# Graph transformer layer pair on one core: reciprocals of the first two graphs due at once, dots of W and a and the check of adj at other times, last unit but one by way of DRAM

## The chip, the cores and the metric

One core of one Trainium2 chip. The metric is the device time of one execution in microseconds (us). All runs quoted are in the fast state. Medians are of the fast runs of one kernel; a ratio is the mean time of one kernel's fast runs over the mean of the other's of the same rounds, so it is not quite the ratio of the medians quoted beside it. Every kernel below gave the right result.

Names: PE is TensorE, DVE VectorE, ACT ScalarE, POOL GpSimd, SP the engine whose queue starts most DMAs. (b, j) is unit j (two heads of eight) of graph b. L648 is line 648 of the kernel. In the profile's names pd is the tile of the sums of the exponentials, ps the scores, po the exponentials times v, pn transposes, pe the product for the diagonal of graph attention, pg graph attention itself; x_, qz_ and y_ with q, k, v, w or y behind them are products with Wq, Wk, Wv, Wo (w) and W (y). Where the prediction says "products of W" at 146.7 us it means those with Wo.

## The reference, cut to what matters

32 graphs of 512 nodes with 512 features go through masked attention and then through graph attention; all is float32.

```python
h = relu(layernorm(x))
q, k, v = h @ Wq + bq, h @ Wk + bk, h @ Wv + bv          # 8 heads of 64
attn = softmax(q k^T / 8 + (1 - adj) * -1e9)
x = x + (attn v) @ Wo + bo
h = relu(layernorm(x)) @ W
e = leaky_relu(h a1 [:, None] + h a2 [None, :]) * adj
x = x + elu(softmax(e) @ h + beta * h)
```

## The kernel before: the parts that the change touches

PE works through a fixed order of parts for each graph. DVE's smaller jobs are not placed by hand: they are put on a list with an earliest time, a deadline and a cost, and a clock that the program keeps while it is built decides where they go. What comes out is a fixed order on each engine.

```python
def pe(us):                      # after each piece of PE work
    clock["pe"] += us
    till = clock["pe"] + (1.0 if at_ends[0] else 0.4)
    while True:
        due = [i for i, (_, t, _) in enumerate(ends) if t <= till]
        fits = [(by, i) for i, (_, t, cost, _, by) in enumerate(spare)
                if max(clock["dve"], t) + cost <= till]
        if due:     ends.pop(due[0])[2]()        # pieces of ACT and POOL that follow
        elif fits:  run_spare(min(fits)[1])      # the piece of DVE with the earliest deadline
        else:       return

def later(key, wait, by, cost, fn):   # earliest time, deadline, cost
    now = max(clock["dve"], clock["pe"])
    spare.append((key, now + wait, cost, fn, now + by))
```

Four kinds of such jobs matter. The check of adj (is every entry 0 or 1?), the dots of W and a (W a1 and W a2, which go to all partitions by way of a row in DRAM), and the reciprocals of the softmax sums:

```python
for t in range(T):                                   # in masks()
    later("bad", 120.0, 200.0, 1.35, lambda t=t: other(t))
...
for c in range(C):                                   # in row_constants()
    for o in range(2):
        later("wa", 40.0, 50.0, 0.75, lambda g=g, c=c, o=o, ar=ar: dot(g, c, o, ar))
...
def finish(b, j, st):
    need("rd")
    if b == B - 1 and j >= NP - 2:
        return finish_last(b, j, st)
    pd = psum.tile([P, N], F32, name=f"pd_{b}_{j}", tag="pd")[:, :H]
    ...                                              # PE: sums of the exponentials into pd
    rd = wtile([P, N], f"rd_{b}_{j}", "rd", 1)       # ONE buffer
    rq = rd[:, :H]

    def divide():
        nc.vector.reciprocal(rq, pd)                 # L638
        then("rd", spread)

    def spread():
        d = dram.tile([2, N], F32, name=f"rd_{b}_{j}", tag="rd")
        nc.scalar.activation(pd, rq, AF.Copy, accum_out=rsum[:, b, j : j + 1])   # L644
        nc.scalar.dma_start(d.rearrange("s (k q) -> (s k) q", k=2), rq[0:P:32, :])
        for s in range(2):
            nc.sync.dma_start(rd[s * HD : (s + 1) * HD, :], d[s : s + 1, :].to_broadcast([HD, N]))
        then("rd", lambda: nc.gpsimd.tensor_tensor(o, o, rd, op=ALU.mult), 6.0)  # L648
    ...
    later("rd", 0.0, gap(b, (j + 1) % NP) - 4.0 if (b, j) != (0, NP - 1) else 0.0, 1.7, divide)
```

The last unit of all (`finish_last`) makes its reciprocals without the trip through DRAM, with two instructions of 1.75 us on DVE. Before, the last but one did so too.

The fourth kind is graph attention's logits: after the eight dots of hn (L767) of a graph, a row goes through DRAM, and DVE makes four logits (L787, L790) and three sums of them (L801). PE needs the last sum for the diagonal (`pe`, part "D"):

```python
nc.vector.scalar_tensor_tensor(z, row, s12[:, 1, k : k + 1], adjT[:, k, :], op0=ALU.add, op1=ALU.mult)  # L787
nc.vector.scalar_tensor_tensor(z, z, ALPHA, z, op0=ALU.mult, op1=ALU.max)                               # L790
...
nc.vector.tensor_tensor(st["as"], st["at"][0] if k == 1 else st["as"], z, op=ALU.add)                   # L801
```

## Time and profile before

| | before |
|---|---|
| median of 3 runs | 3560.45 us (3560.12 to 3561.3) |
| span of the profiled execution | 3561.3 us |
| PE, DVE, ACT, POOL busy | 98, 76, 41, 39% |
| single waits of PE over 3 us | 6.8 (qz_q), 5.1 (pe, end), 4.9 (qz_k), 4.4 (pd), 3.6 (pd, end), 3.3 (qz_y, end) |

PE is the bound over nearly the whole span. All that a change of order can win lies at the two ends, at 150 to 250 us and from 3440 us on. The lines are in the prediction.

### The profile page before, as it was taken

The page shows a single profiled execution, that of the slowest core. Times are in us where ns is not written, and L with a number is a line of the kernel's source. Part 1 is how long each engine was busy: PE and PEld are TensorE (multiplying, and loading weights), DVE is VectorE, ACT ScalarE, POOL GpSimd, SP SyncE. Part 2 cuts the span into 40 slices and gives each one's busy share as a digit, 9 for nine tenths or more (in the row PEclk, how much of TensorE's full clock was granted, in tenths as well). Part 3 has the DMA queues.
Part 4 walks back from the last instruction along what each step waited for, and adds up shares of the span by engine and source line. Part 5 has one row for each costly group of instructions (what it writes and reads, how often), then busy time and mean ns, then how long its engine had stood idle before and what let it go on. Part 6 is the DMA issues. An engine that isn't in the chain of part 4 may idle for free.

```text
span 3561.3 us, 64126 instructions
## 1 busy us (share of the span) xinstructions
PE 3507.7 (98%) x26349; PEld 1887.9 (53%) x26350; DVE 2719.2 (76%) x4209; ACT 1453.1 (41%) x2310; POOL 1390.3 (39%) x1094
## 2 busy tenths in 40 slices
PE   9989999999999999999999999999999999999997
PEld 5545555555555555555555555555555555555543
DVE  6787777787777777777877777777778777778775
ACT  3334443444444344434444444444344444344432
POOL 5232443334443324433334433244433344333442
PEclk9999999999999999999999999999999999999998
DMA  4001111011111011111111110111101111101101
GB/s 137 16 31 45 51 46 37 31 46 48 50 47 37 28 46 52 45 39 31 45 46 51 45 37 28 49 48 45 48 27 41 45 51 46 37 29 48 48 25 34
DMA packets 109227, 154.49 MB, mean 43 GB/s; under 512 B 16456, under 2 KB 54848, under 8 KB 108928
## 3 DMA queue, kind: packets, MB, share of 16 engines
q1 hardware_dynamic: 106336, 147.96, 13.3%
q8 instruction: 210, 3.44, 0.4%
q10 hardware_dynamic: 2384, 2.09, 0.2%
q14 instruction: 89, 0.73, 0.1%
q0 software_dynamic: 208, 0.27, 0.0%
HBM read 116.14 MB, written 34.14 MB: 42 GB/s over the span
## 4 chain that ended last, share of the span: by engine, by line
PE 94%; DVE 3%; DMA 1%; POOL 1%; issue 1%; ACT 0%; SPq 0%; ACTq 0%; POOLq 0%; DVEq 0%
PE ps L558 12%; PE po L609 12%; PE pg L53 12%; PE qz_k L53 5%; PE qz_q L53 5%; PE qz_v L53 5%; PE qz_w L53 5%; PE qz_y L53 4%; PE x_v L53 3%; PE x_k L53 3%; PE x_w L53 3%; PE y_k L53 3%; PE y_v L53 3%; PE y_q L53 3%; PE x_q L53 3%; PE y_w L53 3%
## 5 line engine op out<-in xcount | busy, mean ns | idle before, releaser
L585 ACT ACTIVATE e<-e 128x1024 f32<-128x1024 f32 x512 | 541.4, 1057 | 206.1 <-DVE e L570 169.5
L648 POOL TENSOR_TENSOR oT<-oT,rd 128x512 f32<-128x512 f32 x126 | 177.3, 1407 | 964.6 <-DMA rd<-rd 608.7
L570 DVE SCALAR_TENSOR_TENSOR e<-maskT,ps 128x1024 f32<-128x1024 uint8 x384 | 456.6, 1217 | 94.8 <-PE ps L558 94.6
L558 PE MATMUL ps<-qT,kT 64*128 64x512 f32 x2048 | 476.1, 603 | 3.7 <-DVE e L570 2.0
L609 PE MATMUL po<-e,v 128*64 128x512 f32 x2048 | 464.0, 594 | 0.0
L53 PE MATMUL pg<-at,hn 128*64 128x512 f32 x2048 | 446.9, 594 | 1.9 <-ACT gT L840 1.1
L582 DVE TENSOR_TENSOR es<-es,e 128x1024 f32<-128x1024 f32 x254 | 382.1, 1504 | 10.5
L558 PEld LDWEIGHTS ps<-qT,kT 64*128 64x128 f32 x2048 | 186.1, 186 | 291.2 <-issue 207.0
L501 POOL TENSOR_TENSOR qT<-qT,edge 128x256 f32<-128x256 f32 x128 | 83.8, 676 | 570.3 <-DVE qT L497 570.3
L53 PEld LDWEIGHTS pg<-at,hn 128*64 128x64 f32 x2048 | 145.3, 137 | 288.9 <-issue 279.9
L609 PEld LDWEIGHTS po<-e,v 128*64 128x64 f32 x2048 | 148.5, 138 | 230.3 <-issue 219.3
L862 POOL TENSOR_TENSOR y<-y,x 128x512 f32<-128x512 f32 (+1 forms) x126 | 159.6, 1272 | 188.1 <-DVE y L854 181.6
L688 POOL TENSOR_TENSOR x<-x,c_row 128x512 f32<-128x512 f32 x128 | 182.7, 1448 | 102.2 <-DMA x<-in_x_dram 102.2
L638 DVE RECIPROCAL rd<-pd 128x256 f32<-128x256 f32 x126 | 220.6, 1751 | 0.7 <-issue 0.4
L359 DVE TENSOR_SCALAR x<-x,mv,rs 128x512 f32<-128x512 f32 x128 | 97.4, 804 | 161.9 <-POOL rs L334 161.8
L794 ACT ACTIVATE at<-at 128x512 f32<-128x512 f32 x128 | 80.2, 628 | 294.9 <-DVE at L790 290.8
L767 DVE CUSTOM_DVE_ANT_0 scr<-hn,wa_r 128x512 f32<-128x512 f32 x256 | 169.5, 694 | 36.0 <-ACT hn L754 36.0
L53 PE MATMUL qz_y<-w,vT 128*64 128x256 f32 x1520 | 183.5, 384 | 6.2 <-DVE yq L884 6.2
L582 DVE TENSOR_TENSOR es<-e,e 128x1024 f32<-128x1024 f32 x127 | 187.9, 1480 | 0.0
L852 DVE TENSOR_SCALAR y<-y 128x512 f32<-128x512 f32 x128 | 56.8, 444 | 148.3 <-ACT y L849 148.1
L565 DVE SCALAR_TENSOR_TENSOR e<-maskT,ps 128x512 f32<-128x512 uint8 x256 | 163.6, 681 | 0.0
L840 ACT COPY gT<-pg 128x512 f32<-128x512 f32 x128 | 74.9, 586 | 202.0 <-PE pg L53 199.8
(228 smaller groups left out, 6323.8 us busy)
## 6 DMA issues: line engine op xcount, KB each, us to landing
x<-in_x_dram SPq DMA_DIRECT2D x130, 256.0 KB, 5.5
out_dram<-y SPq DMA_DIRECT2D x128, 256.0 KB, 2.1
rd<-rd SPq DMA_DIRECT2D x252, 128.0 KB, 2.8
x<-in_x_dram SPq DMA_DIRECT2D x62, 512.0 KB, 4.3
s<-row_s SPq DMA_DIRECT2D x32, 256.0 KB, 4.1
rd<-rd ACTq DMA_DIRECT2D x126, 4.0 KB
adj<-in_adj_dram SPq DMA_DIRECT2D x4, 256.0 KB, 4.1
wk<-in_L_gnn_Wk_dram ACTq DMA_DIRECT2D x3, 256.0 KB, 8.1
```

What stands on the lines that cost most here:

```text
L53: nc.tensor.matmul(out[s : s + HD], lhsT[:, s : s + HD], rhs, start=start, stop=stop, skip_group_check=onto)
L558: nc.tensor.matmul(ps[s], st["kT"][j][rows, ts(k, P)], st["qT"][j][rows, :], start=True, stop=True)
L565: nc.vector.scalar_tensor_tensor(e[:, s, :], maskT[:, k, :], NEG, ps[s], op0=ALU.mult, op1=ALU.add)
L570: nc.vector.scalar_tensor_tensor(e, maskT[:, k, :].unsqueeze(1).to_broadcast([P, 2, N]), NEG, p, op0=ALU.mult, op1=ALU.add)
L582: (nc.gpsimd if early else nc.vector).tensor_tensor(es, one, e, op=ALU.add)
L585: nc.scalar.activation(e, e, AF.Exp)
L609: nc.tensor.matmul(po[s * HD : (s + 1) * HD, :], v[k // 2][:, k % 2, (2 * j + s) * HD : (2 * j + s + 1) * HD], e[k][:, s, :], start=k == 0 ...
L638: nc.vector.reciprocal(rq, pd)
L648: then("rd", lambda: nc.gpsimd.tensor_tensor(o, o, rd, op=ALU.mult), 6.0)
L688: nc.gpsimd.tensor_tensor(r[:, t, :], r[:, t, :], c_row, op=ALU.add)
L767: nc.vector.tensor_tensor_reduce(scr, st["hn"][t], r, 1.0, 0.0, op0=ALU.mult, op1=ALU.add, accum_out=st["s12"][:, g, t : t + 1],)
L862: (nc.vector if b == B - 2 else nc.gpsimd).tensor_tensor(yu, yu, x_[:, :, ts(i, H)], op=ALU.add)
```

## The change

Its intent: let the reciprocals of graphs 0 and 1 go at once, so that the single PSUM buffer of the sums and the trips through DRAM don't hold PE; move the other spare jobs out of their way; and at the end take one reciprocal and one multiplication off DVE, by sending the last unit but one through DRAM like all others.

```diff
-            later("bad", 120.0, 200.0, 1.35, lambda t=t: other(t))
+            later("bad", 105.0, 130.0, 1.35, lambda t=t: other(t))
...
-                    later("wa", 40.0, 50.0, 0.75, lambda g=g, c=c, o=o, ar=ar: dot(g, c, o, ar))
+                    later("wa", 46.0, 50.0, 0.6, lambda g=g, c=c, o=o, ar=ar: dot(g, c, o, ar))
...
-        if b == B - 1 and j >= NP - 2:
+        if (b, j) == (B - 1, NP - 1):
             return finish_last(b, j, st)
...
-        later("rd", 0.0, gap(b, (j + 1) % NP) - 4.0 if (b, j) != (0, NP - 1) else 0.0, 1.7, divide)
+        later("rd", 0.0, gap(b, (j + 1) % NP) - 4.0 if b > 1 else 0.0, 1.7, divide)
...
-        pd = psum.tile([P, N], F32, name=f"pd_{b}_{j}", tag=("pd", "po")[j % 2])
+        pd = psum.tile([P, N], F32, name=f"pd_{b}_{j}", tag="po")
...
         def last_sums_behind():
             ...
-            run_all("rd")
```

## The prediction

> **What bounds the kernel now.** I read, in order: the page's busy times and chain, stretches of the time line by engine, the waits of TensorE, then the instructions of each engine around the two ends.
>
> ```profile
> PE 3507.7 (98%) x26349; PEld 1887.9 (53%) x26350; DVE 2719.2 (76%) x4209; ACT 1453.1 (41%) x2310; POOL 1390.3 (39%) x1094
> PE 94%; DVE 3%; DMA 1%; POOL 1%; issue 1%; ACT 0%; SPq 0%; ACTq 0%; POOLq 0%; DVEq 0%
> ```
>
> PE is busy in 3507.7 of 3561.3 us, so everything that waiting can cost is 53.6 us plus slow matmuls after waits. That is the ceiling: 2% would be 71 us.
>
> ```profile
> 150.00:200.00 50.00, 40.73 (x274) 21.77 (x270) 33.72 (x54) 18.67 (x28) 16.22 (x15) 0.90 0.13 43
> 200.00:250.00 50.00, 42.40 (x318) 22.92 (x312) 43.99 (x65) 14.37 (x25) 11.73 (x11) 0.93 0.06 17
> 300.00:350.00 50.00, 50.00 (x400) 28.02 (x400) 38.89 (x66) 23.37 (x36) 10.19 (x11) 1.00 0.11 33
> 3440.00:3460.00 20.00, 15.06 (x112) 8.39 (x108) 18.76 (x31) 7.01 (x11) 3.01 (x2) 0.91 0.11 37
> 3460.00:3480.00 20.00, 15.28 (x112) 10.50 (x112) 17.66 (x21) 7.10 (x16) 16.00 (x11) 0.83 0.16 56
> ```
>
> Columns: stretch, length, busy time of PE, PEld, DVE, ACT, POOL, granted clock, DMA. Between 300 us and 3400 us PE is full and its clock is 1.00; it loses time only at 150-215 us (graphs 0 to 2) and after 3447 us, where the clock also falls and, at the end, DVE is nearly full.
>
> ```profile
> PE qz_q L53 <- ACT qz_q L464: 6.8, 1, 6.8
> PE pe L53 <- DVE x L709: 5.1, 1, 5.1
> PE qz_k L53 <- POOL hT L379: 4.9, 1, 4.9
> PE pd L629 <- ACT pd L644: 4.4, 1, 4.4
> PE pd L658 <- DVE es L582: 3.6, 1, 3.6
> ```
>
> Five single waits make 24.8 us. The engine named is only the last link. From the time lines:
>
> ```profile
> 166.24 1.75 DVE L638 RECIPROCAL rd<-pd 128x256 f32<-128x256 f32 x1
> 168.59 1.08 PE L629 MATMUL pd<-es,ones 128*32 128x256 f32 x8 [4.41 <-ACT pd L644]
> 177.26 1.27 POOL L648 TENSOR_TENSOR oT<-oT,rd 128x512 f32<-128x512 f32 x1 [25.50 <-DMA rd<-rd]
> 187.47 3.57 PE L53 MATMUL qz_k<-hT,wk 128*64 128x256 f32 x16 [4.86 <-POOL hT L379]
> 203.29 0.68 DVE L254 SCALAR_TENSOR_TENSOR sq<-adj 128x512 f32<-128x512 f32 x1
> 210.96 1.75 DVE L638 RECIPROCAL rd<-pd 128x256 f32<-128x256 f32 x1
> 214.06 3.68 PE L53 MATMUL qz_q<-tT,wq 128*64 128x256 f32 x16 [6.75 <-ACT qz_q L464]
> ```
>
> One late reciprocal (graph 1, unit 0; its sums were ready at 144.8) holds the single pd buffer, so PE stops before 168.59. The same reciprocal's trip through DRAM ends at 177.26; POOL stands behind it and then does the blocks of W, so the combination of hT that PE needs is late (187.47). Third, DVE does the check of adj (four pairs, 203.29 to 208.56) and sums before the next reciprocal (210.96); ACT, in order, waits for that reciprocal in front of the copy that PE needs (214.06).
>
> **What the Trainium skill says.** (1) "TensorE: Matmul & The Clock Gate", Part 1: after about 3.4 us idle PE falls to half rate, and takes about 3.4 us of work to leave it. The trace agrees: 16 matmuls of 1.90 us took 3.57 and 3.68 us after 4.86 and 6.75 us idle; after 1.45 us idle they took 1.95. (2) Same page, specification table: the queues of ScalarE and VectorE are strict FIFO. So the place of a reciprocal in the order decides who waits, as above. (3) "VectorE: DVE Perf Modes", "First, the fixed hardware budget": the reciprocal is an iterative divide. The trace agrees: 1751 ns for 256 columns, against 690 ns for a tensor-tensor of 512. (4) "SBUF - State Buffer": VectorE with two SBUF inputs and GpSimd exclude each other on a shared port pair. The trace agrees: a dot of W takes 0.41 us alone and 1.49 us at 136.5-140.7, where POOL adds rows.
>
> **The change, part by part.** Nothing is removed from PE, and steady graphs (b>1) keep their deadlines. The program places spare DVE work by its own running clock and by deadline; I followed that arithmetic by hand for the new numbers.
>
> Reciprocals due at once: the one of (1,0) had a deadline 8 behind, after all 16 dots; now it is first as soon as 1.7 fits, in the second product of W, at about 146.7. Its pd is free by 149, its DRAM trip (5.3 us from 116.5 to 121.83; 9.3 us from 167.9 to 177.26) done by 158. Gone is the 4.41 us wait with the slow matmuls behind it: pd 1.08-0.64, pn 3.68-1.97, po 3.90-3.60, together 2.45. In return the transposes wait about 1.05 us for an eviction, as they do for graph 1 at 70.36. Sum 5.8 us.
>
> Dots later and counted as 0.6: four of them leave the slot at 136-141 and the last ends about 178, so POOL does the combinations of hT (from 169) ahead of the blocks of W. Gone: 4.86 and 3.57-1.90, sum 6.5 us.
>
> Now PE is earlier and DVE has the same work: four statistics of graph 0 have earlier deadlines than the reciprocal of (1,1), which is then forced at the denominators of (1,2). I place its end at 189.1 and PE's arrival at 187.3: a new wait of 2.3 us.
>
> Check of adj earlier: ready in the W products, but fits only behind that reciprocal, ahead of the dots of hn, at 189-194; the reciprocal of (1,2) then comes after ACT's copy. Gone: 6.75, 3.68-1.90 and 2.19-1.90, sum 8.8 us. So far 5.8+6.5-2.3+8.8 = 18.8 us.
>
> Given back: the dots of hn (8 x 0.61 us) are now pushed into the V products of graph 2; the row's trip through DRAM (5.6 us, from 3499.16 to 3504.78) ends about 219, and the four logits (1.37 each) and three sums (0.69) run from 221.7 to 229.1, while PE wants their total at 222.4. Wait 6.8 us, slow matmuls 1.7, less the 0.7 us that PE lost at 247 to the same ops: 7.8 us. Start: 18.8-7.8 = 11.0 us.
>
> End: the last unit but one (31,2) had two reciprocals (3.57) and a multiply (0.69) on DVE at 3441.79, ahead of the sums PE waits for (3.62 us at 3450.96). Now one of 1.75 behind those sums, and the multiply on POOL. The 3.62 wait goes, but PE then waits for the next DVE product (3461.99), and DVE is the bound through 3483. So I count the DVE work removed, 1.82+0.69 = 2.5 us, not 3.62 plus slow matmuls. The new DRAM trip should end by 3453 to 3457; POOL needs the pair only when the last unit is multiplied, about 3456.5. It is hidden, barely.
>
> Total 11.0+2.5 = 13.5 us: 3560.45-13.5 = 3547.0 us.
>
> **Rivals.** A: the wait for the total of graph 0's logits does not appear, since the dots of hn fit earlier than I place them. For: their real duration is 0.61 against 0.8 in the program's clock. Against: order, not duration, puts them there. Start 18.8+, total about 21 us, 3539. B: the waits only move: DVE is 44.0 of 50 us busy in 200-250, and PE gets in its way sooner, so more than one new wait over 3.4 us follows, each with slow matmuls. Start under 5 us, 3554. C: at the end the DRAM trip takes 9.3 us and more and lands on the path; the 2.5 us are lost, 3549.5. D: the whole end gap counts (3.62+1.5) and the DVE chain shortens as POOL's port is free: 5 us, 3544.5.
>
> **Range and chances.** Spread is 1.2 us over three runs, so the range is of mechanism: A and D together give 3537, B gives 3554 to 3556. 3537 to 3555. Faster by 2% would need 71 us, over the whole idle time: 1%. Slower by 2% would need a new stall in every graph, and b>1 is untouched: 1%. Within 2%: 98%.
>
> **What would show it.** Right: reciprocal of (1,0) near 147, no wait at pd of (1,1), at qz_k or at qz_q of graph 2; check of adj before the dots of hn; a 2 us wait at pd of (1,2); a wait of 5 to 8 us at the first pe product near 229; from 300 us on the same pattern shifted by 11 us; at the end one L665 pair and no wait at L658, the qz_y wait starting near 3453 in old time and ending 2.5 us sooner. Wrong: the pd or qz waits still there under another releaser, the logits' total ready in time, or POOL at L392 waiting for the DRAM trip.

## The result, and the profile after

The changed kernel took 3556.89 us (median of 4, 3554.63 to 3558.66) against 3560.28 us for the kernel before (median of 4 by then, 3558.37 to 3561.3); the ratio is 0.9991, 95% interval 0.9973 to 1.0008. That is some 3.4 us less where 13.5 were predicted, and outside the range. Later, with 21 runs: 3557.29 against 3561.17, ratio 0.9989 (0.9983 to 0.9996), 3.9 us less. The two profiled executions took 3563.08 us (2.6 above the median of before) and 3555.89 us (1.0 below the median of after), with spans of 3561.3 and 3554.0 us, so the two profiles differ by twice what the medians do.

The page's busy times and chain, after:

```profile
PE 3500.7 (98%) x26353; PEld 1884.6 (53%) x26354; DVE 2721.7 (77%) x4207; ACT 1452.4 (41%) x2310; POOL 1396.0 (39%) x1095
PE 94%; DVE 4%; DMA 1%; POOL 0%; issue 0%; ACT 0%; ACTq 0%; SPq 0%; DVEq 0%; POOLq 0%
```

The four stretches of the two ends (stretch, length, busy time of PE, PEld, DVE, ACT, POOL, granted clock, DMA share, GB/s):

```profile
150.00:200.00 50.00, 46.36 (x364) 25.86 (x362) 42.41 (x72) 20.76 (x31) 18.49 (x15) 1.00 0.16 43
200.00:250.00 50.00, 36.09 (x248) 17.03 (x246) 44.52 (x63) 14.51 (x22) 15.03 (x11) 0.86 0.06 17
3440.00:3460.00 20.00, 13.20 (x108) 8.30 (x106) 18.70 (x29) 4.78 (x11) 8.67 (x7) 0.83 0.21 54
3460.00:3480.00 20.00, 13.68 (x115) 9.97 (x113) 18.28 (x26) 6.29 (x13) 10.30 (x7) 0.90 0.16 54
```

PE gained 5.63 us of busy time at 150 to 200 us (46.36 against 40.73) and lost 6.31 at 200 to 250 us (36.09 against 42.40). Most of what was won in the first stretch was given back in the second. (Busy time counts slow matmuls in full, so it cannot say how much; PE's start times, below, can.) The waits of PE name the place (total, times, longest):

```profile
PE pe L53 <- DVE as L801: 14.0, 2, 12.6
PE qz_y L53 <- DVE yq L884: 9.6, 2, 6.8
...
PE pd L629 <- ACT pd L644: 2.5, 1, 2.5
...
PE qz_q L53 <- DVE qT L497: 1.1, 1, 1.1
```

The time line of PE shows the same in order: no wait at the sums (1,1), none at qz_k, the new wait at the sums (1,2), and then 12.60 us at the diagonal of graph 0.

```profile
163.78 0.64 PE L629 MATMUL pd<-es,ones 128*32 128x256 f32 x8
...
176.56 1.90 PE L53 MATMUL qz_k<-hT,wk 128*64 128x256 f32 x16
...
189.64 0.64 PE L629 MATMUL pd<-es,ones 128*32 128x256 f32 x8 [2.54 <-ACT pd L644]
...
236.79 1.22 PE L53 MATMUL pe<-ones,as 128*64 128x64 f32 x16 [12.60 <-DVE as L801]
237.80 4.77 PE L609 MATMUL po<-e,v 128*64 128x512 f32 x16
```

PE arrived at the diagonal at 236.79 - 12.60 = 224.19. In the kernel before it arrived at 241.14 and found the sums done at about 235.7: it did not wait at all.

```profile
235.03 0.69 DVE L801 TENSOR_TENSOR as<-as,at 128x512 f32<-128x512 f32 x1
241.14 1.06 PE L53 MATMUL pe<-ones,as 128*64 128x64 f32 x16
```

So PE came 17 us earlier, and DVE's sums came one microsecond **later** (236.73). Why they did is seen on DVE and on POOL of the changed kernel:

```profile
197.97 1.76 DVE L638 RECIPROCAL rd<-pd 128x256 f32<-128x256 f32 x1 [3.02 <-POOL oT L648]
...
225.97 0.74 DVE L787 SCALAR_TENSOR_TENSOR at<-s,s,adjT 128x512 f32<-128x512 f32 x1
226.75 1.64 DVE L790 SCALAR_TENSOR_TENSOR at<-at 128x512 f32<-128x512 f32 x1
228.30 1.75 DVE L787 SCALAR_TENSOR_TENSOR at<-s,s,adjT 128x512 f32<-128x512 f32 x1
...
233.50 3.23 DVE L801 TENSOR_TENSOR as<-as,at 128x512 f32<-128x512 f32 x2
```

```profile
226.14 1.69 POOL L648 TENSOR_TENSOR oT<-oT,rd 128x512 f32<-128x512 f32 x1 [19.42 <-DVE at L790]
227.91 1.60 POOL L378 TENSOR_TENSOR uT<-oT,oT 128x512 f32<-128x512 f32 x1
229.58 1.59 POOL L379 TENSOR_TENSOR oT<-oT 128x512 f32<-128x512 f32 x1
```

From 226.14 on POOL multiplies, combines and adds rows, and from the same moment each instruction of DVE takes 1.6 to 1.75 us instead of 0.69 to 0.74. The starts alternate: POOL 226.14, DVE 226.75, POOL 227.91, DVE 228.30, POOL 229.58. Four logits and three sums took 223.19 to 236.73, 13.5 us. And one reciprocal stood 3.02 us for its single buffer. At the end, the wait at L658 is gone and the one at qz_y has doubled, as predicted:

```profile
3456.18 3.28 PE L53 MATMUL qz_y<-w,vT 128*64 128x256 f32 x16 [6.80 <-DVE yq L884]
```

### The profile page after: what moved, and what is told of

Its sections match the earlier page's. It is cut to its first block, busy times and chain, and to the rows that moved or that the text cites. A ratio compares the mean times of both kernels' runs of the same rounds, so it can differ in the third digit from the quotient of the medians.

```text
span 3554.0 us, 64143 instructions
## 1 busy us (share of the span) xinstructions
PE 3500.7 (98%) x26353; PEld 1884.6 (53%) x26354; DVE 2721.7 (77%) x4207; ACT 1452.4 (41%) x2310; POOL 1396.0 (39%) x1095
## 4 chain that ended last, share of the span: by engine, by line
PE 94%; DVE 4%; DMA 1%; POOL 0%; issue 0%; ACT 0%; ACTq 0%; SPq 0%; DVEq 0%; POOLq 0%
PE ps L558 13%; PE pg L53 12%; PE po L609 12%; PE qz_v L53 5%; PE qz_q L53 5%; PE qz_w L53 5%; PE qz_k L53 5%; PE qz_y L53 4%; PE x_k L53 3%; PE x_v L53 3%; PE x_w L53 3%; PE x_q L53 3%; PE y_q L53 3%; PE y_v L53 3%; PE y_k L53 3%; PE y_w L53 3%
## 5 line engine op out<-in xcount | busy, mean ns | idle before, releaser
L359 DVE TENSOR_SCALAR x<-x,mv,rs 128x512 f32<-128x512 f32 x128 | 108.6, 891 | 159.4 <-POOL rs L334 159.3
```

## The experiments

Each kernel ran in five rounds with the kernel before on the same chip. "Gain" is the median of before in the same rounds less the kernel's own.

| run | what | median us (runs) | before, us | gain | ratio, 95% interval |
|---|---|---|---|---|---|
| p0_after | the changed kernel | 3557.29 (21) | 3561.17 | 3.9 | 0.9989, 0.9983-0.9996 |
| p1_start_only | new start, old end | 3561.02 (13) | 3561.17 | 0.2 | 1.0000, 0.9991-1.0008 |
| p2_end_only | old start, new end | 3559.04 (13) | 3561.17 | 2.1 | 0.9993, 0.9985-1.0002 |
| p4_pool_later | after, POOL held back | 3553.98 (14) | 3561.17 | 7.2 | 0.9981, 0.9973-0.9989 |
| p5_check_early | after, check 30 us sooner | 3562.22 (13) | 3561.59 | -0.6 | 1.0002, 0.9994-1.0011 |
| p6_both_early | p5, first reciprocals sooner | 3561.12 (13) | 3561.59 | 0.5 | 0.9998, 0.9990-1.0006 |
| p7_both_pool_later | p6, POOL held back | 3557.71 (21) | 3561.59 | 3.9 | 0.9988, 0.9981-0.9995 |
| p3b_own_buffer | after, second buffer | 3557.39 (21) | 3561.56 | 4.2 | 0.9988, 0.9981-0.9995 |
| p8_both_own | p6, second buffer | 3557.94 (21) | 3561.56 | 3.6 | 0.9990, 0.9984-0.9997 |
| p9_both_own_later | p8, POOL held back | 3553.64 (12) | 3561.56 | 7.9 | 0.9978, 0.9969-0.9986 |
| p10_own_later | p3b, POOL held back | 3553.50 (10) | 3561.56 | 8.1 | 0.9977, 0.9968-0.9987 |
| p11_root_first | p9, root ahead of a product | 3547.43 (5) | 3562.35 | 14.9 | 0.9957, 0.9944-0.9971 |
| p12_rd_only | before, reciprocals alone | 3565.34 (13) | 3562.35 | -3.0 | 1.0008, 1.0000-1.0017 |
| p13_dots_only | before, dots alone | 3562.78 (13) | 3562.35 | -0.4 | 1.0000, 0.9992-1.0009 |
| p14_check_only | before, check of adj alone | 3556.74 (21) | 3562.35 | 5.6 | 0.9985, 0.9979-0.9992 |

The theory: the start's gain is lost where PE waits for graph 0's sums, because DVE's instructions there are stretched by POOL and come late from DVE's own queue. Rivals: the end went wrong; the single rd buffer did it; waits only trade places, so that nothing in this stage can win.

### The two ends apart: p0_after, p1_start_only, p2_end_only

p0 is the changed kernel, unedited. p1 takes back the three edits of the end, p2 the three of the start.

> The changed kernel again, unedited, for five rounds. If the 3.4 us gain of the first four runs is real and not spread, it is 2.5 to 5 us below the kernel before here too, about 3556.5 us. A new profile should show the same pattern as the first: the wait at the first pe product of graph 0 between 11 and 14 us, the wait at pd of (1,2) near 2.5 us.

> The changed kernel with its end put back: both last units divided in place at the end, all reciprocals run in the last step. Only the deadlines at the start differ from before. Theory (start and end are independent, start worth 3.7 us at the x_w products of graph 1 in the profiles): 3556.5 us, 3 to 4.5 us below before, and the wait of 3.6 us at L658 is back. Rival (the gain is all from the end): 3560, no gain.

> The kernel before with the new end alone. My prediction gave 2.5 us for it. Theory (DVE is the bound from 3440 to 3483, so what counts is DVE work removed, 2.5 us): 2 to 3.5 us below before, about 3557.5, no wait at L658, the wait at the qz_y product near 6.8 us. Rival (the whole 3.6 us wait and the slow matmuls behind it count): 5 us below, 3555. Second rival (lost in spread or to the DRAM trip): under 1 us.

The end alone is worth 2.1 us; 2.5 were predicted, and the interval holds both that and zero. The start alone is worth 0.2 us, and with the new end it is worth 3.9 - 2.1 = 1.8; the intervals are some 3 us wide to each side. So the start, of which 11.0 us were expected, gives 0 to 2 us by the medians. The end is cleared.

### POOL held back: p4_pool_later

```diff
-            then("rd", lambda: nc.gpsimd.tensor_tensor(o, o, rd, op=ALU.mult), 6.0)
+            then("rd", lambda: nc.gpsimd.tensor_tensor(o, o, rd, op=ALU.mult), 1000.0 if (b, j) == (1, 3) else 6.0)
...
         def U():
+            if b == 2:                     # 4 columns, reads graph 0's sums
+                gate = wtile([P, T], "gate", "gate", 1)
+                nc.gpsimd.tensor_tensor(gate, old["as"][:, :T], mhalf, op=ALU.add)
             need("rd")
```

> The changed kernel with one added POOL instruction of 128x4 that reads the sum of graph 0's logits, ahead of the multiply of (1,3), the combinations of oT and the rows of graph 1; so these POOL operations start only when the logits' sums are done. Theory (in the changed kernel the eleven DVE operations of logits and sums took 13.4 us from 223.2 to 236.7 instead of 7.4 since POOL used the shared port in the same time): they take about 7.5 us, the wait at pe falls from 12.6 to 6.5 us, the whole run is 4 to 6 us faster than the changed kernel, about 3551.5. Rival (the wait is set by when the dots of hn and the row's trip through DRAM are done, not by the port): the wait stays above 11 us and the time at 3556.5.

It gained 3.3 us on the changed kernel of the same rounds. DVE's time line, then PE's:

```profile
226.94 0.69 DVE L790 SCALAR_TENSOR_TENSOR at<-at 128x512 f32<-128x512 f32 x1
...
229.73 1.49 DVE L801 TENSOR_TENSOR as<-as,at 128x512 f32<-128x512 f32 x2
```

```profile
231.27 1.23 PE L53 MATMUL pe<-ones,as 128*64 128x64 f32 x16 [6.89 <-DVE as L801]
```

With POOL still, the same logits and sums took 223.38 to 231.2, 7.8 us instead of 13.5, and the wait fell from 12.7 to 6.89, to what the prediction had put there (6.8). So of the wait in the changed kernel about 5.8 us is the stretch. It is worth less than that. From p0 to p4 PE passed the diagonal 6.3 us sooner, but it began the next products with Wo only 4.1 us sooner (283.21 and 279.07). POOL's work now falls on the four instructions of the diagonal itself, which took 5.69 us instead of 1.53, and a wait of 1.08 us follows at the next scores. (The profiled execution of p4 is the fastest of its 14; the medians give the 3.3 us.) The gate was tried in four kernels, with and without the other edits, and was worth much the same each time: 3.3 (p0 to p4), 3.4 (p6 to p7), 4.3 (p8 to p9) and 3.9 us (p3b to p10).

### The single buffer: p3b_own_buffer

A first kernel for this was refused by the build (one pool tag with two sizes). In its successor every engine's order is that of the changed kernel.

```diff
-        rd = wtile([P, N], f"rd_{b}_{j}", "rd", 1)
+        rd = wtile([P, N], f"rd_{b}_{j}", "as" if (b, j) == (1, 2) else "rd", 1)
```

> The changed kernel, every engine's order the same, with a buffer of its own for the reciprocal of (1,2) (the one of the row of a, free by then, that the sums take later), so that VectorE no longer waits there until GpSimd has multiplied by the reciprocals of (1,1). What I hold: the 3.0 us of VectorE's wait go, and the TensorE wait of 1.1 us at the last q product where it was; the wait at the diagonal of graph 0 stays at 11 to 13 us, since the stretched logits and sums set it, so 3556.3 to 3557.3, 0 to 1 us below the changed kernel. The rival, that this buffer is a main part of what the prediction left out, expects the wait at the diagonal to fall by 3 us and about 3553.

As expected: 0.3 us more gain than the changed kernel had, and the wait at the diagonal is 12.9. DVE no longer waits at that reciprocal (2.63 us in p0), and PE simply waits longer at the diagonal. The wait of 1.1 us at qz_q is gone too, but p0's profile, of the unedited kernel, has none either: PE came later there, behind slow matmuls. The rival fell, for this kernel.

### Take DVE's backlog away: p5_check_early, p6_both_early, p7_both_pool_later

```diff
-            later("bad", 105.0, 130.0, 1.35, lambda t=t: other(t))
+            later("bad", 75.0, 200.0, 1.35, lambda t=t: other(t))        # p5, p6, p7
...
-        later("rd", 0.0, gap(b, (j + 1) % NP) - 4.0 if b > 1 else 0.0, 1.7, divide)
+        later("rd", 0.0, gap(b, (j + 1) % NP) - 4.0 if b > 1 else -30.0, 1.7, divide)   # p6, p7
```

p7 has the gate of p4 as well.

> The changed kernel with the four pieces of the check of adj made ready 30 us sooner on the kernel's own clock, so that they fall into VectorE's idle time before 140 us. VectorE is then freed of 5.4 us between 183 and 197 us. What I hold (the wait at the diagonal is VectorE's backlog at 180 to 230 us, plus the stretch by GpSimd): dots of hn, first logit and the rest come 4 to 5 us sooner, the wait at the diagonal falls from 12.7 to 7 to 9 us; 3553 against 3557. The rival, that the backlog is only moved and the wait stays at 12 us or over, expects 3556 to 3557.

> The same, and the reciprocals of the first two graphs given a deadline 30 us sooner, so that the one of (1,1) comes ahead of dots and statistics: the wait of 2.5 us at the sums (1,2) goes, and the wait of VectorE for the single buffer at the reciprocal of (1,2). Expected: wait at the diagonal of graph 0 of 4 to 8 us, no wait over 1 us at the sums (1,2); 3551, that is 6 us below the changed kernel. The rival, that waits only trade places in this stage, expects the sum of TensorE's waits between 140 and 300 us to stay within 2 us of the changed kernel's, and 3555 to 3557.

> The same, and GpSimd's multiplication (1,3), combinations and rows held back until graph 0's sums are done (as in the run that held them back in the changed kernel, which was worth 3.3 us and took the wait at the diagonal from 12.7 to 6.9). If the two causes add up: wait at the diagonal of 1 to 3 us and 3548, or some 12 us below the kernel before. If the backlog was only ever the stretch, nothing more than that run had: 3554.

My expectations missed all three by 9 to 10 us, and the rivals written beside them by 4 to 5. DVE did get the 5.3 us of the check out of its way and the wait at the diagonal fell to 9.3 us, but a wait of 5.4 (p5) or 9.0 us (p6) came up earlier, at y_q. What held PE there in p5 is on DVE:

```profile
198.95 1.76 DVE L638 RECIPROCAL rd<-pd 128x256 f32<-128x256 f32 x1 [8.69 <-POOL oT L648]
```

and behind it on POOL:

```profile
197.65 1.26 POOL L648 TENSOR_TENSOR oT<-oT,rd 128x512 f32<-128x512 f32 x1 [8.35 <-DMA rd<-rd]
```

The chain: the row of W a2 goes to DRAM and back through SP's queue. In p6 its second DMA (L138) stood until 191.05, 8.5 us after the first (182.57), and the DMA of the reciprocals of (1,1) stood behind it in the queue (191.55), however early the reciprocal itself had been. So POOL's product came at 197 us, and DVE, without other work in front of it, ran straight into the one rd buffer. The 3.02 us of the changed kernel were the tip of this: there the check of adj happened to fill the time. ACT stood behind DVE, and PE behind ACT's copy.

### The same with the buffer: p8_both_own, p9_both_own_later, p10_own_later

> The run with the check and the first reciprocals early, with that buffer added. There VectorE stood 9.0 us at the reciprocal of (1,2), which waited for the multiplication by the reciprocals of (1,1) at 197.4, and ScalarE and TensorE stood behind it (wait of 9.0 us at y_q). If the single buffer is what spoilt that run: the wait at y_q falls below 2 us, the wait at the diagonal stays at or below 9.3 us, and the time falls by 7 to 9 us, to 3552 to 3554. If the waits only move to the next place, the sum of TensorE's waits from 140 to 300 us stays at 19 to 22 us and the time at 3559 to 3561.

> The same with GpSimd's multiplication (1,3), combinations and rows held back until graph 0's sums are done: wait at the diagonal of 1 to 5 us and 3548 to 3551, below every kernel so far. If the holding back gives nothing once the rest is in order, the same as the run without it, within 1 us.

> The changed kernel with the buffer of its own and GpSimd held back, without the early check and reciprocals. If the buffer matters only beside the stretch: 1 to 3 us below the run that only held GpSimd back (3554), so 3551 to 3553, with a wait at the diagonal of 4 to 6 us. If it doesn't matter, 3553.5 to 3554.5 and 6.9 us.

With the buffer p8 gained 3.1 us on p6 (3.6 less 0.5), not the 7 to 9 that I expected: a wait of 5.5 us took the place of the 9.0. p9 came out 3 us above its range; p10, expected at 3551 to 3553 if the buffer mattered, has 3553.5 and an unchanged 6.9 us at the diagonal. p9, with all edits, was no faster than p10, which has no earlier check. In p9 DVE stands here:

```profile
198.89 0.16 DVE L749 SCALAR_TENSOR_TENSOR nb<-mv,rs 128x2 f32<-128x2 f32 x1 [8.06 <-POOL rs L334]
```

It waits for a square root of two columns on POOL (0.70 us, at 198.16), and that stood in POOL's queue behind the same product by the reciprocals of (1,1), which waited 9.64 us for its DMA.

### The last link: p11_root_first

```diff
-            then("rd", lambda: nc.gpsimd.tensor_tensor(o, o, rd, op=ALU.mult), 1000.0 if (b, j) == (1, 3) else 6.0)
+            then("rm" if (b, j) == (1, 1) else "rd", lambda: nc.gpsimd.tensor_tensor(o, o, rd, op=ALU.mult),
+                 {(1, 1): 14.0, (1, 3): 1000.0}.get((b, j), 6.0))
...
         def U():
+            run_all("rm")
```

> As p9_both_own_later, but GpSimd's multiplication by the reciprocals of (1,1), which waited 9.6 us for a DMA, comes behind the second square root of graph 0's statistics, which stood behind it from 189 to 198 us. If that order is what made the wait of 5.8 us at the last q products: that wait falls below 1.5 us, VectorE's 8.1 us idle at the nb instruction goes, the wait at the diagonal stays within 2 us of 5.4, and the time falls by 4 to 7 us to 3547 to 3550. If VectorE's sum of work to the diagonal is the limit, the wait at the diagonal grows by what the other loses (to 8 us or over) and the time stays at 3552 to 3554.

Since order on the other engines follows from the program's clock, a few DVE and ACT instructions between 186 and 230 us changed places too: the next reciprocal now stands ahead of the statistics, and dots go between the evictions of q. POOL's time line, and PE's:

```profile
192.11 1.60 POOL L334 TENSOR_TENSOR rs<-rs,mhalf 128x2 f32<-128x2 f32 x1 [4.15 <-DVE rs L333]
198.08 3.12 POOL L648 TENSOR_TENSOR oT<-oT,rd 128x512 f32<-128x512 f32 x2 [4.37 <-DMA rd<-rd]
```

```profile
200.03 1.90 PE L53 MATMUL qz_q<-tT,wq 128*64 128x256 f32 x16
...
228.62 1.23 PE L53 MATMUL pe<-ones,as 128*64 128x64 f32 x16 [6.81 <-DVE as L801]
```

The wait of 5.8 us at qz_q is gone, as is DVE's idle time at nb, and the one at the diagonal grew by 1.4. Because of the instructions that moved along, the run shows what this order is worth, 7.0 us on p9, and not the root alone. The kernel took 3547.43 us, 14.9 less than the kernel before and some 11 less than the changed one, by the gains of their own rounds. It beats both. It is five fast runs from 3547.07 to 3548.17; the runs of before in these rounds spread over 6 us.

### One edit of the start at a time: p12_rd_only, p13_dots_only, p14_check_only

Each is the kernel before with one line of the change.

> The kernel before with the deadline of the first two graphs' reciprocals alone. The wait of 4.4 us at the sums (1,1) shrinks or goes; the later waits stay or grow, since the dots and the check still stand in VectorE's queue. VectorE's sums of graph 0's logits end at 235.6 in the kernel before and at 236.7 in the changed one: what I hold now is that this end moves by less than 3 us under any single edit, so that the time is 3559 to 3562.5, no more than 2 us below the kernel before. The prediction's own reading would make it 5 us below, 3556.

> The kernel before with the other time and cost of the dots of W and a alone. Expected 3559 to 3563, within 2 us of the kernel before; the wait at the sums (1,1) may shrink by the 1 to 3 us that dots stood ahead of the reciprocal of (1,1), and what it gives comes back at the next wait for VectorE. The prediction's own reading would find some of its 18.8 us here, 2 us or more.

> The kernel before with the other time of the check of adj alone. The check's 5.3 us stand at 203.3 to 208.6 in the kernel before, right ahead of the reciprocal and of the evictions of q, where TensorE waits 6.8 us: that wait falls by 4 to 6 us if the check comes earlier into idle time, and the time is 3556 to 3559; or, if what it gives comes back at the diagonal as in the changed kernel, 3559.5 to 3562.

The dots alone do nothing (the three old waits stand at 4.4, 4.8 and 6.0). The reciprocals alone **cost** 3.0 us by the medians, though the interval just reaches zero: more than I had held possible. The trace (of the slowest of the 13 runs, 4.3 us above their median) puts it on the buffer, as in p5; no run gave this kernel a second one:

```profile
198.00 1.76 DVE L638 RECIPROCAL rd<-pd 128x256 f32<-128x256 f32 x1 [8.54 <-POOL oT L648]
```

```profile
200.94 3.68 PE L53 MATMUL y_q<-tT,wq 128*64 128x256 f32 x16 [7.27 <-ACT y_q L453]
```

PE passed the diagonal at 245.15 in that kernel (241.14 in the kernel before), after a wait of 9.34 us. The check alone is worth 5.6 us by the medians, more than the 3.9 of the whole change; but the intervals, some 3 to 7 and 1 to 6 us, overlap, so that it is more is not shown:

```profile
207.28 1.90 PE L53 MATMUL qz_q<-tT,wq 128*64 128x256 f32 x16
...
235.21 1.23 PE L53 MATMUL pe<-ones,as 128*64 128x64 f32 x16 [2.69 <-DVE as L801]
```

The wait of 6.75 us at qz_q is gone with its slow matmuls, the two earlier waits stay (4.42 and 4.99), and at the diagonal 2.69 us are given back.

## Why the prediction was wrong, point by point

**The end: right.** 2.5 us predicted, 2.1 measured in p2. The wait at L658 went and qz_y's grew from 3.30 to 6.80, since DVE is the bound there. POOL's product of (31,2) started at 3452.90 and the trip through DRAM stayed hidden.

**The start until 212 us: right in place and nearly in size.** I compare PE's start times before and after, less the 0.32 us by which the changed kernel was ahead at 140 us.

| step of the prediction | predicted | measured | from PE's times |
|---|---|---|---|
| wait at the sums (1,1) gone | +5.8 | +5.3 | first po behind: 173.20, 167.57 |
| wait at qz_k gone | +6.5 | +7.0 | y_k behind: 190.88, 178.29 |
| new wait at the sums (1,2) | -2.3 | -2.6 | x_q behind: 200.18, 190.21 |
| wait at qz_q gone | +8.8 | +7.7 | po behind: 221.27, 203.64 |
| lead at the po of (1,3) | 18.8 | 17.3 | |

The step of 8.8 lost 1.1 us to a wait of 1.08 at qz_q which I had not seen (the single rd buffer); in p14, without it, the same step shows whole: 221.27 - 212.46 = 8.8.

**"Given back": the step that failed.** I put 7.8 us there. The lead fell from 17.3 at the po of (1,3) to 3.4 us at the first product with Wo of graph 1 (285.68 and 281.97, less 0.32): 13.9 us given back. The prediction let DVE run its logits and sums from 221.7 to 229.1, in 7.4 us, with POOL out of the picture. They ran from 223.19 to 236.73. So they began 1.5 us late and took 6.1 us more. PE arrived 1.8 us later than predicted (224.19 instead of 222.4), so the wait came out at 12.6 instead of 6.8. p4 shows the cause of 5.7 of the 6.1: with POOL held back the same instructions took 7.8 us and the wait was 6.89. The rest is slow matmuls (po 4.77 against 3.61) and one late wait of 1.14 us at 280 us. I had quoted the shared port myself, with a dot of 1.49 us instead of 0.41 (in the trace POOL was making the combinations of oT at the first two of these dots and began to add rows only near the third), but asked only what POOL does to DVE where it stood before. I did not ask what POOL would do at the new time. POOL's product (1,3), combinations and rows come free when the reciprocal of (1,3) comes, and that moved forward too, from 235.64 to 217.76, so that they now fell onto the logits. (The profile names DVE's L790 as the last releaser of that product; that it is the DMA of the reciprocals, issued at 221.37, is inferred: the same product is released by it in the kernel before, at 242.77, and in p5.)

**What the sum cannot show.** The terms are right one by one as far as 212 us, yet they don't belong to the edits that I gave them to. I gave 5.8 and 6.5 us to reciprocals and dots. Alone these edits cost 3.0 us (the interval just reaches zero) and nothing, and the check alone gives 5.6. PE's lead is worth only what the sums of graph 0 allow, and in the kernel before PE reached the diagonal some 5.5 us after them (241.14 and 235.7). That slack is what an edit that leaves DVE's sums where they are can win; the check alone wins just it. Everything beyond needs the sums themselves sooner, as in p4 (231.2) and p11 (228.6).

**The rivals.** B (waits only move, 3554) came nearest, with the right mechanism in the wrong number: it asked for more than one new wait over 3.4 us, and it was one. A (no wait at the diagonal) is refuted, and so is C: POOL's product of (31,2) waited for DVE, not for the trip through DRAM. D (the whole end gap, 5 us) is unlikely with 2.1 us in p2, though the interval just reaches it.

**What stays open.** The parts do not quite add up in time: the start lead of the profiled executions (3.4 us for the changed kernel, 7.1 for p4) plus 2.1 for the end is 5.5 and 9.2, while the medians give 3.9 and 7.2. And one and the same start gave 1.8 us with the new end and 0.2 with the old one. For the two profiled executions the place can be seen. At the diagonal p0 and p1 have the same lead over the kernel before (4.0 us each, once the 0.45 us by which both were behind it at 145 us is taken off); at the next products with Wo p0 has 2.9 left and p1 only 0.3. In between, at one instruction, p0's DVE started ahead of POOL and p1's just behind it:

```profile
277.75 0.43 DVE L852 TENSOR_SCALAR y<-y 128x512 f32<-128x512 f32 x1
277.97 1.34 POOL L862 TENSOR_TENSOR y<-y,x 128x512 f32<-128x512 f32 x1 [1.34 <-DVE y L854]
```

```profile
277.94 1.26 POOL L862 TENSOR_TENSOR y<-y,x 128x512 f32<-128x512 f32 x1 [1.34 <-ACT y L849]
277.98 1.51 DVE L852 TENSOR_SCALAR y<-y 128x512 f32<-128x512 f32 x1 [0.18 <-issue]
```

The first pair is p0, the second p1. DVE's 0.43 us became 1.51; in p1 PE then waited 1.31 us (y, L854), and its next scores and sums ran slow. So, as far as two traces show it, a difference of some tenths of a microsecond in who comes first was worth 2.6 us. How often it falls either way in the unprofiled runs, and whether it makes the difference of the medians, no run shows.

## What to carry to other kernels

Before you add up waits that a change removes, find the next thing that the waiting engine needs and ask when it can be there at the earliest. The gain ends at that time, here the sums of graph 0. Work that comes free sooner also collides sooner: when a change moves a reciprocal forward, follow its consumers on the other engines, and look whom they meet at their new time. And a product that waits for a DMA at the head of an in-order queue blocks whatever small thing stands behind it; putting a root of two columns ahead of one, with what moved along, was worth 7 us, nearly as much as all the other edits of that kernel.

## What the Trainium skill lacked or had wrong

- "SBUF — State Buffer", in its section on the two separate sides, says that VectorE (with two SBUF inputs) and GpSimd exclude each other on the shared port pair: whichever starts first has it for its whole instruction, and the other blocks. The trace agrees, but the page does not say how the blocking looks in a profile: as longer **busy** time, not as idle. DVE's 0.69 and 0.74 us became 1.64 and 1.75 us with no idle time shown, and POOL's 1.27 became 1.6 to 1.7. DVE's busy share thus rises where it is being held up.
- "TensorE: Matmul & The Clock Gate", Part 1, gives about 3.4 us of idle time for the fall to half rate and says that the number of slow matmuls varies from run to run. Here 16 matmuls of normally 1.90 us took 1.95 in one execution of the changed kernel and 3.39 in another, behind the same wait of 2.54 us. A wait well below 3.4 us can thus cost slow matmuls or not.
